# Query and output projections as seven products of blocks, and weight sums moved to GpSimd, in a float32 macaron block

## The chip, the cores and the metric

One core of one Trainium2 chip. The metric is device time in microseconds (us) of one execution: the median of several runs.

## The reference: what is computed

A block with two feed-forward halves around an attention, each with a residual, for 8 samples of 512 tokens by 512 features, all in float32:

```python
x = x + 0.5 * ffn(layernorm(x), w_gate, w_up, w_down)
x = x + attn(layernorm(x), W_q, W_k, W_v, W_o)
x = x + 0.5 * ffn(layernorm(x), w_gate, w_up, w_down)

# ffn: 512 -> 2048 -> 512
h = silu(x @ w_gate) * (x @ w_up)
h = keep the two largest magnitudes of every four of h
return h @ w_down

# attn: 16 query heads and 4 key/value heads of 32 features, rotary positions
Q, K, V = x @ W_q, x @ W_k, x @ W_v
out = softmax(rope(Q) @ rope(K).T / sqrt(32)) @ V
return out @ W_o
```

## The kernel before

**Engines.** TensorE (PE in the profile) multiplies; VectorE (DVE) and ScalarE (ACT) read its banks; [...] SyncE's queue (SP) issues every DMA in one order. A float32 matmul appears as two instructions, so four matmuls are eight rows.

**Stages.** The work is a row of 16 feed-forward blocks (`blocks`, two for each sample), and `ffn` (L503) is the main stream: four chunks of 512 hidden features, two groups each. A group is computed by `woven` (L593) as seven products of quarter blocks in place of eight (a Strassen-Winograd scheme: sums of quarters of the tokens and of the weights are multiplied, the results are added and subtracted by VectorE). A product is four matmuls of 128x128 by 128x256, issued at L604; weights come as 16 quarters ahead of use (`load_quarters`, L106). After a chunk, `keep_two_of_four` (L371) makes the mask on VectorE and three sums on GpSimd (L424 to L429). Then `products` (L513) multiplies two chunks by down weights, in seven products of eight matmuls (L532), which VectorE adds to the tokens (L545). Down weights need sums of quarters; `combine_down` (L469) makes them once, in the first block: it loads `raw` (L473), VectorE adds (L482), and SP stores each sum to DRAM (L483). The sums for gate and up weights are made in the first block as well, by `combine_gu` (L668; additions at L673, stores at L674).

**What goes between.** Layer norms and attentions are generators that the main loop at L1018 advances a step at a time between feed-forward products. Each has a place in the count `n` of feed-forward steps (`sides`, L974): a step runs when `n` has passed its due and its operands are ready by the plan, or when it is 3 steps late. So the order on every engine is written when the kernel is built. The plan keeps a clock for each engine (`at`, L141). VectorE work that can wait stands in three queues (`soon`, urgent; `later`; `for_later`), from which `fill` (L352) issues what fits behind TensorE's clock. `ensure` issues what must be out.

**Attention** (`attention`, L752) for a sample: load `wqkv` (all of W_q, W_k and W_v in one tile), norm and transpose; `projected` (L768) makes keys, then each quarter of the queries by four matmuls of 128x512 (L772), and VectorE rotates each part (a shuffle, two products, an addition); values at L797. Then, for each of the four quarters of the heads, `scores` (L813; four banks `sc` that VectorE reduces to maxima), `exponentials` (L845), `weighted` (L862) and `divided` (L878). At the end the outputs: four matmuls of 128x512 for each 128 tokens (L944), added to the tokens by VectorE (L951) and stored (L952). The four PSUM banks of `sc` and of `st` are one slot; three more banks serve all other products, one serves `ops`. `p_slots` are two SBUF tiles of 1 MB that attention shares with `raw`.

Of the kernel before, what the change touches and what calls it, by code (L numbers as in the profile page):

```python
# [26 lines left out]
def macaron_block(  # L27
# [31 lines left out]
    wap = ctx.enter_context(tc.tile_pool(name="wap", bufs=1))  # L59
    qkvp = ctx.enter_context(tc.tile_pool(name="qkvp", bufs=1))  # L60
# [140 lines left out]
    wa_slots = Slots(wap, "wa", 1)  # L201
# [54 lines left out]
    def layernorm_t(got, tag, src=None, xb=None):  # L256
# [3 lines left out]
        xn = []  # L260
        for t in range(NT):
            xn.append(xnp.tile([P, D], FP, tag=tag, name="xn"))
            if xb is None:
                nc.sync.dma_start(out=xn[t], in_=src[t * P : (t + 1) * P, :])
# [36 lines left out]
        def sums():  # L301
# [3 lines left out]
            got["sums"] = ts = tp.tile([P, 4, 2, HALF], FP, tag="ts", name="ts")  # L305
            got["made"] = [
                later(0.62, partial(nc.vector.tensor_tensor, ts[:, i], a, b, ALU.subtract), at["act"])
# [3 lines left out]
        if xb is None:  # L311
# [19 lines left out]
            if tag == "xf":  # L331
                sums()
# [113 lines left out]

    gu_made, written = {}, {}
# [21 lines left out]
    def combine_down():  # L469

        for c in range(NCH):
# [6 lines left out]
            sums = wa_slots.tile([P, 6, 2, HD2], FP, "sums")  # L478

            def combine(i, name, c=c, quarter=quarter, sums=sums):  # L480
                op = ALU.add if name[2] == "+" else ALU.subtract
                nc.vector.tensor_tensor(sums[:, i], quarter[name[:2]], quarter[name[3:]], op)  # L482
                nc.sync.dma_start(out=combined[c // 2, name][:, c % 2 * 2 : c % 2 * 2 + 2, :], in_=sums[:, i])  # L483

            for i, name in enumerate(SUMS):
                made = later(0.7, partial(combine, i, name), at["pe"], for_later)
            p_slots.used(wa_slots.used(made))
            yield now
        ensure([made])
# [13 lines left out]
    def ffn(b, final, last):  # L503
# [9 lines left out]
        def products(hs, g):  # L513

            operands = []

# [234 lines left out]

    def attention(b):  # L752
        ensure(written[b, 0])
        wa = wa_slots.tile([P, ND, D + 2 * KV], FP, "wqkv")
        for src, col in ((w_k, D), (w_q, 0), (w_v, D + KV)):
            nc.sync.dma_start(
                out=wa[:, :, col : col + src.shape[1]], in_=src.rearrange("(c p) n -> p c n", p=P)
            )
        cs = p_slots.tile([P, 4, S], FP, "cs")
        nc.sync.dma_start(out=cs[:, :2, :], in_=rope.rearrange("a p s -> p a s"))  # L760
        got = {}
# [6 lines left out]
        def projected(dst, col, scale):  # L768

            ps = Bank([P, S], "proj")  # L770
            for k in range(ND):
                nc.tensor.matmul(  # L772
                    out=ps.tile, lhsT=wa[:, k, col : col + P], rhs=xT[:, k, :], start=(k == 0), stop=(k == ND - 1)
                )
            takes("pe", 3.62)
            fill()
            sw = w_slots.tile([P, S], FP, "sw")
            soon(0.65, partial(nc.vector.stream_shuffle, sw, ps.tile, SWAP))
            read = soon(
                0.62, partial(nc.vector.scalar_tensor_tensor, dst, ps.tile, scale, cs[:, 0, :], ALU.mult, ALU.mult)  # L780
            )
            ps.free([read])
            soon(0.65, partial(nc.vector.scalar_tensor_tensor, sw, sw, scale, cs[:, 1, :], ALU.mult, ALU.mult))
            made = soon(0.65, partial(nc.vector.tensor_tensor, dst, dst, sw, ALU.add))
            return [p_slots.used(w_slots.used(made))]

        of_k = projected(kT, D, 1.0)
        yield now
        of_q = []
        for c in range(ND):  # L790
            of_q.append(projected(qT[:, c, :], c * P, 1.0 / math.sqrt(HD)))
            yield now
        ensure(of_q[-1])
        vps = Bank([P, NT, KV], "vps")
        for t in range(NT):
            for k in range(ND):
# [3 lines left out]
                    rhs=wa[:, k, D + KV : D + 2 * KV],  # L800
# [5 lines left out]
        in_xT.remove(got)  # L806
        nc.scalar.copy(v, vps.tile)
        vps.free(end=takes("act", 0.6, pe_heard()))
        wo = wa_slots.tile([P, ND, D + 2 * KV], FP, "wo")
        nc.sync.dma_start(out=wo[:, :, :D], in_=w_o.rearrange("(c p) n -> p c n", p=P))  # L810
        yield partial(when, of_k + of_q[0])
# [88 lines left out]
        ensure(of_k + of_q[0])  # L900
# [33 lines left out]
        xts = []  # L934
        for t in range(NT):
            xts.append(xnp.tile([P, D], FP, tag="xa", name="xt"))
            nc.sync.dma_start(out=xts[t], in_=tokens[b][1][t * P : (t + 1) * P, :])
        out_of = divided(*last)
        yield partial(when, out_of)
        ensure(out_of)  # L940
        for t, xt in enumerate(xts):
            y = Bank([P, D], "y")
            for k in range(ND):
                nc.tensor.matmul(  # L944
                    out=y.tile, lhsT=qT[:, k, t * P : (t + 1) * P], rhs=wo[:, k, :D], start=(k == 0), stop=(k == ND - 1)
                )
            takes("pe", 3.65)
            fill()

            def add(t=t, xt=xt, y=y):  # L950
                nc.vector.tensor_tensor(xt, y.tile, xt, ALU.add)  # L951
                nc.sync.dma_start(out=tokens[b][2][t * P : (t + 1) * P, :], in_=xt)  # L952

            made = [soon(0.62, add)]
            y.free(made)
            if t == NT - 1:
                ensure(made)
# [132 lines left out]
```

## Time and profile before

| what | value |
|---|---|
| median of 3 runs (lowest to highest) | 3263.59 us (3262.45 to 3264.31) |
| the profiled execution: its time | 3262.97 us |
| its span, first to last instruction | 3261.2 us |
| mean granted TensorE clock | 0.997 |
| TensorE, VectorE, ScalarE, GpSimd busy | 3200.0, 2261.7, 1196.7, 564.3 us |
| VectorE rows of 128x512 float32 | 0.67 to 0.80 us each |
| 256 KB of gate/up weights, issue to landing (median) | 3.3 us |

How to read it: durations are of one profiled execution. A row of the timeline gives its start, how long it lasted, the engine, the line, the operation, what it writes and reads, and how many instructions are merged in it; in brackets stands idle time before it and who ended it. Ends of matmuls are modelled and overlap the next start, so how long TensorE takes for a piece is read from start to start. The view of waits names who waited for whom: total, times, longest. One block of the main stream is some 200 us long, the first block is the first 125 us or so together with the sums of weights.

### The profile page before, as it was taken

What the parts mean: (1) busy time and instruction counts of PE and PEld (TensorE: products, weight loads), DVE (VectorE), ACT (ScalarE), POOL (GpSimd) and SP (SyncE); (2) the same over time, 40 slices, a digit from 0 to 9 for tenths busy, and PEclk for the clock granted to TensorE, in tenths of its full rate; (3) what the DMA queues carried; (4) which work ended last, traced back from release to release, by engine and by line L of the source; (5) the groups of instructions that cost most, each with busy time, mean ns of one, the idle gap of its engine ahead of it and who ended that gap; (6) DMA issues with size and microseconds to landing.
All of it is one profiled execution on the core that took longest, in us unless ns stands there. A gap on an engine that the chain in (4) does not pass through costs nothing.

```text
span 3261.2 us, 43693 instructions
## 1 busy us (share of the span) xinstructions
PE 3200.0 (98%) x15880; PEld 2316.7 (71%) x15880; DVE 2261.7 (69%) x4892; ACT 1196.7 (37%) x1686; POOL 564.3 (17%) x868
## 2 busy tenths in 40 slices
PE   7999999999999999999999999999999999999999
PEld 5786667766667677766776668766766678666886
DVE  6767775778577775776578865777577765777554
ACT  2222552155324451354314442155325542255221
POOL 0221112210130112110221111211120121201120
PEclk9999999999999999999999999999999999999999
DMA  7563334543433444334453345433533436234451
GB/s 244 196 221 108 116 127 145 174 130 101 158 134 126 136 139 162 133 118 138 143 172 129 110 154 176 140 119 117 196 97 115 155 126 210 91 117 135 156 174 46
DMA packets 249285, 463.21 MB, mean 142 GB/s; under 512 B 24432, under 2 KB 64368, under 8 KB 248304
## 3 DMA queue, kind: packets, MB, share of 16 engines
q1 hardware_dynamic: 249072, 460.42, 42.9%
q8 instruction: 127, 2.08, 0.3%
q14 instruction: 86, 0.70, 0.1%
HBM read 421.53 MB, written 38.80 MB: 141 GB/s over the span
## 4 chain that ended last, share of the span: by engine, by line
PE 92%; DVE 4%; DMA 2%; ACT 1%; issue 0%; POOL 0%; SPq 0%; DVEq 0%; ACTq 0%
PE x L604 25%; PE y L532 23%; PE v L604 12%; PE z L604 6%; PE proj L772 4%; PE sc L817 4%; PE st L850 4%; PE ops L865 4%; PE y L944 3%; PE tr L244 1%; PE gu L579 1%; DMA xn<-x 1%; DVE nm L157 1%; PE den L883 1%; PE vps L797 1%; PE y L562 1%
## 5 line engine op out<-in xcount | busy, mean ns | idle before, releaser
L604 PE MATMUL x<-ts,w 128*128 128x256 f32 x3000 | 721.5, 383 | 10.7 <-DVE corner L618 9.2
L604 PEld LDWEIGHTS x<-ts,w 128*128 128x128 f32 x3000 | 560.0, 190 | 165.5 <-issue 50.1
L532 PE MATMUL y<-wd,h 128*128 128x256 f32 x1984 | 457.3, 385 | 12.0 <-DVE h L418 6.3
L532 PEld LDWEIGHTS y<-wd,h 128*128 128x128 f32 x1984 | 375.8, 192 | 101.3 <-issue 32.0
L858 ACT ACTIVATE p<-st 128x2048 f32<-128x2048 f32 x128 | 239.6, 1872 | 400.7 <-PE st L855 233.2
L424 POOL TENSOR_TENSOR e<-h 128x512 f32<-128x512 f32 x62 | 89.3, 1440 | 1615.4 <-DVE h L418 1442.7
L157 DVE TENSOR_REDUCE nm<-sc 128x1 f32<-128x512 f32 x512 | 320.2, 681 | 68.8 <-PE sc L817 66.9
L532 PE MATMUL y<-wd,e 128*128 128x256 f32 x1488 | 337.3, 381 | 0.2 <-PE den L883 0.2
L545 DVE SCALAR_TENSOR_TENSOR x<-y,x 128x512 f32<-128x512 f32 x372 | 241.9, 683 | 130.2 <-PE y L532 128.6
L532 PEld LDWEIGHTS y<-wd,e 128*128 128x128 f32 x1488 | 279.7, 190 | 62.3 <-issue 18.7
L236 ACT ACT_TABLE_LOAD x216 | 277.1, 1283 | 4.5 <-PEq L1079 0.7
L224 ACT COPY row<-x 128x512 f32<-128x512 f32 x212 | 124.1, 585 | 392.5 <-PE x L604 392.1
L157 DVE TENSOR_TENSOR p<-p 128x512 f32<-128x512 f32 x384 | 248.4, 700 | 10.4 <-PE ops L865 10.4
L653 ACT ACTIVATE h<-x 128x256 f32<-128x256 f32 x125 | 47.5, 380 | 558.1 <-PE x L604 525.0
L604 PE MATMUL v<-xT,w 128*128 128x256 f32 x1000 | 241.5, 385 | 5.7 <-DVE corner L226 5.7
L604 PE MATMUL v<-ts,w 128*128 128x256 f32 x1000 | 240.1, 383 | 1.1 <-DVE h L157 1.1
L604 PE MATMUL x<-xT,w 128*128 128x256 f32 x1000 | 240.5, 383 | 0.0
L604 PE MATMUL z<-xT,w 128*128 128x256 f32 x1000 | 240.0, 383 | 0.0
L604 PEld LDWEIGHTS v<-xT,w 128*128 128x128 f32 x1000 | 187.3, 191 | 57.3 <-issue 13.2
L604 PEld LDWEIGHTS x<-xT,w 128*128 128x128 f32 x1000 | 185.3, 190 | 57.4 <-issue 30.6
L604 PEld LDWEIGHTS v<-ts,w 128*128 128x128 f32 x1000 | 186.8, 190 | 54.8 <-issue 20.8
L604 PEld LDWEIGHTS z<-xT,w 128*128 128x128 f32 x1000 | 185.8, 190 | 52.6 <-issue 22.9
(106 smaller groups left out, 4010.4 us busy)
## 6 DMA issues: line engine op xcount, KB each, us to landing
w<-gu SPq DMA_DIRECT2D x472, 256.0 KB, 3.3
w<-in_w_gu SPq DMA_DIRECT2D x394, 256.0 KB, 3.3
wd<-wd SPq DMA_DIRECT2D x155, 512.0 KB, 3.8
wd<-in_w_down SPq DMA_DIRECT2D x124, 256.0 KB, 5.0
x<-x SPq DMA_DIRECT2D x64, 256.0 KB, 2.6
xn<-x SPq DMA_DIRECT2D x64, 256.0 KB, 7.0
x<-in_x SPq DMA_DIRECT2D x32, 256.0 KB, 3.4
gu<-w SPq DMA_DIRECT2D x32, 256.0 KB, 2.6
```

Of the source, the lines that this page charges most:

```text
L157: self.does()
L224: nc.scalar.copy(dst, src)
L236: nc.scalar.activation(dummy[:, 1:2], dummy[:, 0:1], f)
L532: nc.tensor.matmul(out=y.tile[:, t, :], lhsT=part[:, t * P : (t + 1) * P], rhs=operands[i][:, n, :], start=(n == 0), stop=(n == 3),)
L545: nc.vector.scalar_tensor_tensor(to, y.tile, 0.5 * sign, to, ALU.mult, ALU.add)
L604: nc.tensor.matmul(out=bank.tile[:, m, :], lhsT=lhs[:, m, k, :], rhs=rhs[:, k, :], start=(first and m == 0 and k == 0), stop=(k == 1), ski ...
L772: nc.tensor.matmul(out=ps.tile, lhsT=wa[:, k, col : col + P], rhs=xT[:, k, :], start=(k == 0), stop=(k == ND - 1))
L817: nc.tensor.matmul(out=sc[:, kv, :], lhsT=qT[rows, c, t * P : (t + 1) * P], rhs=kT[rows, :], start=True, stop=True)
L850: nc.tensor.matmul(out=st[:, kv, :], lhsT=kT[rows, t * P : (t + 1) * P], rhs=qT[rows, c, :], start=True, stop=False)
L858: nc.scalar.activation(p, st, AF.Exp)
L865: nc.tensor.matmul(out=ops[rows, :], lhsT=v[:, t, rows], rhs=p[:, kv, :], start=(t == 0), stop=(t == NT - 1))
L944: nc.tensor.matmul(out=y.tile, lhsT=qT[:, k, t * P : (t + 1) * P], rhs=wo[:, k, :D], start=(k == 0), stop=(k == ND - 1))
```

## The change

1. *Queries and outputs by seven products.* `seven` replaces the four groups of `projected` for queries and the four output groups: seven products of four matmuls of 128x256, accumulated in three banks of the slot of the scores. Between products of one bank VectorE reads it. Each product takes its own weight tile (256 KB) from a new pool `waq` of four, loaded when an earlier one has been used. `b` blocks and their sums (`ts`, now made for attention too) are the tokens' side; for outputs VectorE makes four sums of `qT`.
2. *Rotation by quarters.* Query parts are rotated where they lie in `qT`, as two rows of 256 tokens at a time; the last part straight from the bank.
3. *Order.* Values are projected before the queries; scores begin when all queries are rotated. The attention has 73 steps instead of 65.
4. *Sums by GpSimd.* `combine_down` uses `nc.gpsimd` for its 20 sums, in two parts at other places of the count (11 to 18, 22 to 32, instead of 9 to 25). A new `combine_qo` (36 to 48) makes four sums for W_q and four for W_o by GpSimd, once, and stores them to DRAM.
5. *Buffers.* `wqkv` becomes a tile for keys and values; the four token tiles of an attention become one. The host lays W_q and W_o out in quarters.

```diff
-        for c in range(NCH):
+        for c in range(2 * g, 2 * g + 2):
             raw = p_slots.tile([P, 4, D], FP, "raw")
             nc.sync.dma_start(out=raw, in_=w_down[c])
...
+            for i, name in enumerate(SUMS):
                 op = ALU.add if name[2] == "+" else ALU.subtract
-                nc.vector.tensor_tensor(sums[:, i], quarter[name[:2]], quarter[name[3:]], op)
-                nc.sync.dma_start(out=combined[c // 2, name][:, c % 2 * 2 : c % 2 * 2 + 2, :], in_=sums[:, i])
...
+                total = waq.tile([P, 2, HD2], FP, tag="waq", name="total")
+                nc.gpsimd.tensor_tensor(total, quarter[name[:2]], quarter[name[3:]], op)
+                nc.sync.dma_start(out=combined[g, name][:, c % 2 * 2 : c % 2 * 2 + 2, :], in_=total)
...
+    def combine_qo():
+        for which, how in (("q", Q_SUMS), ("o", O_SUMS)):
+            both = [p_slots.tile([P, 4, 2, HALF], FP, "both") for _ in range(2)]
+            w = [both[q // 4][:, q % 4] for q in range(8)]
+            for q in range(4):
+                nc.sync.dma_start(out=w[q].rearrange("p a b -> p (a b)"), in_=flat(qo_raw[which][q]))
+            there = at["pe"] + 12.0
+            yield lambda: there
+            for to, a, b, op in how:
+                nc.gpsimd.tensor_tensor(w[to], w[a], w[b], op)
+            nc.sync.dma_start(out=qo_sums[which], in_=both[1])
+            yield now
...
+        def seven(lhs, rhs, take):
+            sc = sc_slots.tile([P, N_KV, 2, HALF], FP, "seven")
+            x, v, z = (sc[:, i] for i in range(3))
+            for i, bank in enumerate((x, v, x, v, x, z, x)):
+                w = weights.popleft()
+                for m in range(2):
+                    for k in range(2):
+                        nc.tensor.matmul(
+                            out=bank[:, m, :],
+                            lhsT=lhs(w, i, m, k),
+                            rhs=rhs(w, i, k),
+                            start=(i in (0, 1, 5) and m == 0 and k == 0),
+                            stop=(k == 1),
+                            skip_group_check=True,
+                        )
+                takes("pe", 1.83)
+                if coming_qo:
+                    weights.append(load_qo(*coming_qo.popleft()))
+                fill()
+                entries = take(i, bank)
+                for entry in entries:
+                    sc_slots.used(entry)
+                yield partial(when, entries)
+                takes("pe", 0.0, ensure(entries) + TOLD)
...
+            if i < 3:
+                return [copy((left, corner, right)[i])]
+            if i == 6:
+                return rotate(below, 0, bank)
+            to, j = ((right, 1), (corner, 1), (left, 0))[i - 3]
+            entry = into(to)
+            rotate(to, j)
+            return [entry]
...
-        for t, xt in enumerate(xts):
-            y = Bank([P, D], "y")
-            for k in range(ND):
-                nc.tensor.matmul(
-                    out=y.tile, lhsT=qT[:, k, t * P : (t + 1) * P], rhs=wo[:, k, :D], start=(k == 0), stop=(k == ND - 1)
-                )
-            takes("pe", 3.65)
...
+        def take_output(i, bank):
+            def add(to):
+                nc.vector.tensor_tensor(to, bank, to, ALU.add)
+                if i >= 5:
+                    for t in (0, 1) if i == 5 else (2, 3):
+                        nc.sync.dma_start(out=tokens[b][2][t * P : (t + 1) * P, :], in_=xt[:, t, :])
+            return [soon(0.62, partial(add, (left, corner, right, right, corner, left, below)[i]))]
...
-    sides = [(9, 25, 3 * NCH, combine_down, None, None)]
+    sides = [(11, 18, 6, partial(combine_down, 0), None, None), (22, 32, 6, partial(combine_down, 1), None, None), (36, 48, 4, combine_qo, None, None)]
```

## The prediction

> **What bounds the kernel now.** I read the busy times and the 40 slices first, then TensorE's own waits, then the stages that the change touches in the timeline.
>
> ```profile
> PE 3200.0 (98%) x15880; PEld 2316.7 (71%) x15880; DVE 2261.7 (69%) x4892; ACT 1196.7 (37%) x1686; POOL 564.3 (17%) x868
> ...
> PE   7999999999999999999999999999999999999999
> ...
> PE 92%; DVE 4%; DMA 2%; ACT 1%; issue 0%; POOL 0%; SPq 0%; DVEq 0%; ACTq 0%
> ```
>
> TensorE (PE) is busy nine tenths or more in every slice but the first, and the chain that ended last is 92% TensorE. So taking a matmul away shortens the run as long as the engines that feed TensorE don't turn the gap into a wait. The waits of TensorE alone tell how much waiting there is (columns: total us, times, longest):
>
> ```profile
> PE x L604 <- DVE corner L618: 9.2, 4, 3.7
> ...
> PE sc L817 <- DVE nm L157: 6.9, 7, 1.4
> PE y L532 <- DVE h L418: 6.3, 2, 3.3
> PE v L604 <- DVE corner L226: 5.7, 1, 5.7
> ```
>
> They are few, and the long ones lie in the first block. TensorE's timeline shows stops of 3.74 us (before 54.75), 5.74 (81.19), 3.33 (101.34) and 2.95 (118.57), 15.8 us in all, all released by VectorE (DVE). After each, TensorE runs slower for a while: the eight instructions at 54.75 take 3.44 us, where the same group takes 1.89 elsewhere. That adds 1.55, and in the same way about 1.9, 2.0 and 2.0 us after the other three: 7.4. The first block loses 23 us that way. In the stages that the change rewrites there is no TensorE wait at all:
>
> ```profile
> 261.62 3.60 PE L772 MATMUL proj<-xT,wqkv 128*128 128x512 f32 x8
> 265.05 3.62 PE L532 MATMUL y<-wd,h 128*128 128x256 f32 x16
> 268.51 3.60 PE L772 MATMUL proj<-xT,wqkv 128*128 128x512 f32 x8
> 271.94 1.89 PE L604 MATMUL x<-ts,w 128*128 128x256 f32 x8
> 273.67 3.60 PE L772 MATMUL proj<-xT,wqkv 128*128 128x512 f32 x8
> ```
>
> Starts count here, since ends overlap: a projection group (four 128x512 matmuls, each two instructions) lasts 265.05 - 261.62 = 3.43 us, a feed-forward group of four 128x256 lasts 273.67 - 271.94 = 1.73 us. The output groups at L944 run from 499.03 to 502.46, again 3.43.
>
> [...] the slow groups follow exactly the four long stops. [...]
>
> ```profile
> 78.54 1.71 POOL L427 TENSOR_TENSOR e<-h 128x512 f32<-128x512 f32 x1
> 79.05 1.49 DVE L157 TENSOR_TENSOR h<-h,corner 128x256 f32<-128x256 f32 x1
> ```
>
> The VectorE product has a mean of 0.44 us, and takes 1.49 while GpSimd works.
>
> **The change, part by part.** Sums are made against the profiled execution's 3262.97 us (span 3261.2), 0.6 below the median 3263.59.
>
> 1. *Fewer products.* Queries: four groups of 3.43 = 13.72 us per sample become seven of 1.73 = 12.11. Outputs the same. The saving is 1.61 us a time, 16 times (8 samples, two projections): **25.8 us**, all on the path, because TensorE sets the end there. Weight loads stay in step (190 ns each, beneath matmul halves of 216 ns). Keys and values keep their matmuls (one group of 3.43, and 16 of 128x128); values only move ahead of the queries.
>
> 2. *VectorE per sample.* Removed: 16 query instructions and 4 output additions. Added: 4 sums of xT, 3 copies, 3 additions, 4 rotations of 4 (shuffle, two products, addition), 4 sums of the attention output, 7 output additions: 37 against 20. Rows of 128x512 take 0.67 to 0.73 us, so 17 x 0.69 = 11.7 us a sample, 94 in all; VectorE goes from 2262 to about 2340 us (72%). I put it beside TensorE's work at nothing: in 270 to 290 us, amid the query stage, VectorE is busy 12.4 of 20, in 500 to 520, amid the outputs, 5.4 of 20. If that cover is gone, all 94 could come onto the path (rival 3).
>
> 3. *The new wait.* Each of the 112 products of the seven goes into a bank that VectorE must first have read: copy or addition (0.69 us) behind the product. [...] In the built program's instruction order each of the seven is followed by at least one feed-forward group (1.73 us; often 3.45), so about 1 us is left over for a reader; rotations (about 2.6 us) are queued behind the addition that the next product waits for, but ahead of the one after it. The trace doesn't show this wait in these stages. Lower end: the same scheme in the feed-forward part waits 17.5 us in all at L604, 9.5 of it in the two first-block stops, the other 8 over some 826 products, 0.01 each, 1 us for 112. Below nothing is excluded: no wait stands in these stages that could go. Upper end: one stop of 1.38 us (the usual one before scores) in each of 16 phases: 22. I take **+6**: one 0.75 us stop, as before 909.80, in every second phase.
>
> 4. *Sums of down weights on GpSimd.* Twenty instructions at L482 (0.757 us, 15.1 together) leave VectorE in the first block; GpSimd gets them at 1.27 to 1.44 us (rows L427, L424), 25 to 29 us, and 8 more for query and output weights. [...] from 76.3 to 83.3 us five GpSimd instructions stretched VectorE by about 0.73 + 1.07 + 1.55 = 3.35 us, 0.67 each. 20 x 0.67 = 13.4, so VectorE's net relief is about 2 us. What changes more is the order of transfers on SP. The first stop came from weights issued at 41.16 that landed at 50.8 (in the chain, 7.91 us of that load), just behind a raw load of 1 MB:
>
> ```profile
> 40.64 0.42 SPq L473 DMA_DIRECT2D raw<-in_w_down  x1
> 41.16 2.32 SPq L114 DMA_DIRECT2D w<-in_w_gu  x4
> 43.57 3.28 SPq L483 DMA_DIRECT2D wd<-sums  x4
> ```
>
> In the changed order the second raw load stands behind those four. So I take away the first stop with its slow group (3.74 + 1.55 = 5.3) and half of the third (5.3 / 2 = 2.7), which had five L482 rows just ahead of the instruction awaited: **-8**. The second and fourth I leave: there `h` and mask work is late, and GpSimd now adds to it. Ends: -23 (all stops go) and +13 [...].
>
> 5. *What else is queued.* SP's stores of GpSimd's sums wait for GpSimd, five in a row (some 7 us), and gate/up loads emitted behind them wait as long; in the changed order one such row precedes the loads of the fifth and of the sixth group. Covered by a group's 12 us (seven of 1.73), else in the +13. In attention four large weight loads become 16 of 256 KB, 12 more a sample, about 0.5 us of SP each, past gate/up loads that run up to 16 quarters ahead. Each weight is loaded four products ahead, four times at least 3.46 = 13.8 us, against 3.3 us to land: hidden. The norm's ScalarE and GpSimd steps stay; its small GpSimd chain may stand behind two or three sums (about 4 us) once, within its 13 steps. Scores now wait for all four query parts instead of the first; feed-forward groups fill that: nothing.
>
> Sum: 3262.97 - 25.8 + 6 - 8 = 3235.2; against the median **3236 us**.
>
> **Rivals.**
> 1. *The first block's stops all vanish.* -25.8 - 23 + 3 gives 3217. For it: VectorE released every one. [...]
> 2. *The pairwise exchange eats most of the gain.* A stop of 1.38 us in every phase (22 us) and 4 us off the first block leaves 3263 - 25.8 + 22 - 4 = 3255. For it: VectorE already makes scores wait 1.4 us at a time. Against: no wait in these stages now.
> 3. *VectorE becomes the bound around the rotations and seven pairwise readers* (slower). Each sample adds 11.7 us of VectorE work; the mask steps it pushes back must be done before the down products. It decides from 27% of the 94 us on the path (25.8 / 94; 0.2% slower needs 34%); at half: 3263 - 25.8 + 47 = 3284. For it: slices where VectorE is at eight tenths. Against: 12.4 and 5.4 of 20 us where the work is put.
> 4. *No net change*: a fifth to a third of those 94 us on the path, 3263.
>
> **How the numbers follow.** About 0.2% (6.5 us) is what a measurement of this kernel can tell from no change, so faster is below 3257 and slower above 3270. Forecast (3226 to 3247) 0.60; rival 1 (below 3226) 0.13; rival 2 (3247 to 3257) 0.14; rival 4 0.06; rival 3 0.07. Faster: 0.60 + 0.13 + 0.14 = 0.87. The range runs to the first two rivals: 3216 to 3256, with some 0.17 outside.
>
> **What would show it.** Right: `seven` groups 1.73 us apart, TensorE busy down by about 26 us, hardly any `PE seven <- DVE` wait, no stop before 55 us, VectorE near 2340. Wrong: `PE seven` or `PE y <- DVE h` waits of tens of us (rivals 2, 3), half-clock groups in the first block still, or GpSimd rows above 1.7 us with VectorE rows doubled beside them.

## The result, and the profile after

| | before | after |
|---|---|---|
| median of 5 runs each, on one chip (lowest to highest) | 3263.58 us (3261.74 to 3264.31) | 3293.52 us (3289.91 to 3296.36) |
| ratio, with its 95% interval | | 1.0093 (1.0078 to 1.0107) |
| the profiled execution: its time, its span | 3262.97, 3261.2 us | 3289.91, 3288.1 us |
| mean granted TensorE clock | 0.997 | 0.996 |

The changed kernel is 0.9% slower, where 0.8% faster was predicted. From the page of the changed kernel, the same three parts as were shown of before (busy times, TensorE's slices, the chain that ended last):

```profile
PE 3194.5 (97%) x16264; PEld 2391.3 (73%) x16264; DVE 2380.0 (72%) x5018; ACT 1160.9 (35%) x1636; POOL 614.0 (19%) x896
...
PE   8999999999999999999999999999999999999999
...
PE 84%; DVE 10%; DMA 2%; ACT 2%; issue 1%; POOL 1%; SPq 0%; DVEq 0%; ACTq 0%; POOLq 0%
```

The first slice rose from 7 to 8: the first block gained. Everywhere else the slices look as before; a digit is too coarse for a loss of 1%. The chain tells more: TensorE's share fell from 92% to 84%, VectorE's rose from 4% to 10%. TensorE's waits in the changed kernel (total us, times, longest):

```profile
PE sc L923 <- DVE nm L158: 15.4, 13, 2.0
PE x L608 <- DVE corner L622: 14.0, 7, 5.1
PE x L608 <- ACT row L224: 7.6, 2, 6.0
...
PE ops L971 <- ACT p L964: 4.8, 6, 1.8
...
PE seven L834 <- DVE qT L158: 2.0, 5, 0.5
```

The wait that the change adds, `seven`, is only 2.0 us. What grew is a wait between instructions that the diff doesn't touch: scores waiting for maxima (`sc <- nm`) went from 6.9 us in 7 stops to 15.4 in 13. The stage that was rewritten looks as the prediction said, groups of 1.73 us from start to start, one stop of 0.24:

```profile
279.78 1.89 PE L834 MATMUL seven<-xT,waq 128*128 128x256 f32 x8
281.50 3.62 PE L536 MATMUL y<-wd,e 128*128 128x256 f32 x16
285.36 1.99 PE L834 MATMUL seven<-ts,waq 128*128 128x256 f32 x8 [0.24 <-DVE qT L158]
287.19 3.62 PE L536 MATMUL y<-wd,e 128*128 128x256 f32 x16
```

The first block has no stop at 54.75 us any more; one of 3.58 comes at 67.08, with a group of usual length behind it:

```profile
52.98 1.89 PE L608 MATMUL x<-xT,w 128*128 128x256 f32 x8
54.70 1.89 PE L608 MATMUL v<-ts,w 128*128 128x256 f32 x8
...
67.08 1.99 PE L608 MATMUL x<-ts,w 128*128 128x256 f32 x8 [3.58 <-DVE corner L622]
```

The sums there of GpSimd (POOL), a VectorE row beside them, and SP's stores (GpSimd's, VectorE's and SP's timelines of the changed kernel):

```profile
58.40 6.28 POOL L489 TENSOR_TENSOR total<-raw 128x512 f32<-128x512 f32 x4
```

```profile
60.65 4.57 DVE L677 TENSOR_TENSOR w<-w 128x512 f32<-128x512 f32 x3 [1.67 <-DMA w<-in_w_gu]
```

```profile
38.54 1.84 SPq L115 DMA_DIRECT2D w<-in_w_gu  x4
40.48 8.60 SPq L490 DMA_DIRECT2D wd<-total  x5
...
50.60 0.55 SPq L481 DMA_DIRECT2D raw<-in_w_down  x1
```

Three VectorE sums take 4.57 us beside GpSimd's, where three of the mean length of before take 2.05 (3 x 0.684): the kind of cost that the prediction counted from 76.3 to 83.3 us of the kernel before (3.35 us; the trace has four GpSimd instructions there, not five, so 0.84 each and 16.8 for twenty). SP stands 8.60 us over five stores (some 7 were expected). The four weight loads at 38.54 now go ahead of the second load of `raw`, where they stood just behind it before. The first block is shorter in spite of the two costs.

### The profile page after: what moved, and what is told of

It reads as the page before. It is cut to its first block, busy times and chain, and to the rows that moved or that the text cites. A ratio compares the mean times of both kernels' runs of the same rounds, so it can differ in the third digit from the quotient of the medians.

```text
span 3288.1 us, 44735 instructions
## 1 busy us (share of the span) xinstructions
PE 3194.5 (97%) x16264; PEld 2391.3 (73%) x16264; DVE 2380.0 (72%) x5018; ACT 1160.9 (35%) x1636; POOL 614.0 (19%) x896
## 4 chain that ended last, share of the span: by engine, by line
PE 84%; DVE 10%; DMA 2%; ACT 2%; issue 1%; POOL 1%; SPq 0%; DVEq 0%; ACTq 0%; POOLq 0%
PE x L608 23%; PE y L536 21%; PE v L608 11%; PE z L608 6%; PE seven L834 5%; PE sc L923 4%; PE ops L971 4%; PE st L956 4%; DVE nm L158 2%; PE den L989 1%; PE gu L583 1%; PE tr L244 1%; DVE p L158 1%; ACT p L964 1%; PE vps L866 1%
## 5 line engine op out<-in xcount | busy, mean ns | idle before, releaser
L158 DVE TENSOR_TENSOR p<-p 128x512 f32<-128x512 f32 x384 | 257.9, 726 | 13.4 <-PE ops L971 13.4
```

What stands on the lines that cost most here:

```text
L158: self.does()
```

## Where the time went, stage by stage

The waits listed don't add up to the loss, since many are under the limit of what that view lists, and a stop shows in the length of the next group too (287.19 - 285.36 = 1.83 us behind the stop of 0.24 above, where 1.73 is usual). So I took every group of TensorE from its own start to the next one's, and subtracted what such a group usually takes: 0.216 us for each 128x256 instruction, 0.429 for 128x512, 0.134 for one of `sc`, and so on for each shape, as the undisturbed groups of the trace show. What is subtracted is called work here, the remainder stops. The middle of an attention runs from its first `sc` to its last `den`; its first part, "the first four scores", ends where the first product for exponentials (`st`) starts. Feed-forward groups that lie in a stage count in it. All eight attentions together, us:

| stage | before: work | stops | after: work | stops |
|---|---|---|---|---|
| up to the first keys, first block included | 217.6 | 32.5 | 217.7 | 21.1 |
| keys, values, queries | 274.8 | 0.7 | 341.2 | 8.4 |
| middle: the first four scores of each attention | 189.7 | 16.7 | 174.2 | 40.2 |
| middle: the rest | 1535.9 | 68.4 | 1437.8 | 91.0 |
| outputs | 198.0 | 1.1 | 274.3 | 1.7 |
| between the attentions | 682.7 | 12.4 | 627.4 | 22.3 |
| sum | 3098.7 | 131.8 | 3072.6 | 184.7 |

Some 31 us complete the spans: what lies ahead of TensorE's first group, and everything from the start of its last one on. Of the middles' stops more than 40 us in either kernel are remainders of under 0.3 us at a change of group, which come back in every kernel; the comparison is what counts. The work fell by 26.1 us, as predicted. The stops grew by 53: 46 in the middles (23.5 in the first scores, 22.6 in the rest), 10 between the attentions, 8 at the queries, less 11 up to the first keys. The columns of work show something else: the stages of queries and outputs *grew*, by 66.4 and 76.3 us, although their own products shrank by 26. So 169 us of other work, nearly all of it feed-forward, moved into them: 114 out of the middles and 55 from between.

How that makes stops is seen at the first scores of one attention. In the kernel before (TensorE's timeline):

```profile
295.83 1.14 PE L817 MATMUL sc<-kT,qT 32*128 32x512 f32 x8
296.90 3.72 PE L532 MATMUL y<-wd,e 128*128 128x256 f32 x16
300.55 1.14 PE L817 MATMUL sc<-kT,qT 32*128 32x512 f32 x8
301.62 3.72 PE L532 MATMUL y<-wd,e 128*128 128x256 f32 x16
305.27 1.14 PE L817 MATMUL sc<-kT,qT 32*128 32x512 f32 x8
```

and in the changed kernel, the same scores of the same attention:

```profile
298.91 1.14 PE L923 MATMUL sc<-kT,qT 32*128 32x512 f32 x8
299.98 1.99 PE L608 MATMUL x<-xT,w 128*128 128x256 f32 x8
302.66 1.14 PE L923 MATMUL sc<-kT,qT 32*128 32x512 f32 x8 [0.68 <-DVE nm L158]
303.73 1.99 PE L608 MATMUL v<-ts,w 128*128 128x256 f32 x8
306.41 1.14 PE L923 MATMUL sc<-kT,qT 32*128 32x512 f32 x8 [0.68 <-DVE nm L158]
```

VectorE's side of the changed one:

```profile
300.12 2.48 DVE L158 TENSOR_REDUCE nm<-sc 128x1 f32<-128x512 f32 x4 [0.41 <-PE sc L923]
303.87 2.48 DVE L158 TENSOR_REDUCE nm<-sc 128x1 f32<-128x512 f32 x4 [1.26 <-PE sc L923]
```

A score group needs all four banks of its slot, so it may start only when the four reductions of the one before are done, which take 2.48 us here. Before, 16 instructions of a down product stood between two scores and hid that; after, 8 instructions are left. Other groups had been drawn to the queries and outputs; it is also another moment of the feed-forward block, so this one place doesn't show how much of its difference is the one and how much the other. A score comes every 3.75 us with 2.80 us of TensorE work: 0.95 lost a time. VectorE isn't full here (it stands 1.26 us of the 3.75); each engine waits for the other.

## The experiments

The table has the measured numbers of all runs; middle columns as above. "Steps" are those of one attention. Ratios are against the kernel before on the same chip.

| kernel | steps | median us | ratio (95% interval) | first scores: work / stops | rest: work / stops | queries, outputs: stops | between: stops |
|---|---|---|---|---|---|---|---|
| before | 65 | 3263.58 | 1 | 190 / 16.7 | 1536 / 68.4 | 1, 1 | 12 |
| after | 73 | 3293.52 | 1.0093 (1.0078, 1.0107) | 174 / 40.2 | 1438 / 91.0 | 8, 2 | 22 |
| e3_busywork | 65 | 3264.23 | 1.0006 (0.9997, 1.0014) | 190 / 16.7 | 1536 / 68.3 | 2, 1 | 14 |
| e2_squeeze | 65 | 3261.23 | 0.9996 (0.9988, 1.0005) | 216 / 7.1 | 1491 / 75.1 | 1, 1 | 16 |
| e5_squeeze_more | 65 | 3270.50 | 1.0024 (1.0015, 1.0033) | 221 / 6.8 | 1408 / 91.4 | 2, 1 | 6 |
| e1_pace | 73 | 3277.40 | 1.0047 (1.0032, 1.0062) | 147 / 36.3 | 1485 / 94.5 | 8, 2 | 9 |
| e4_norm_first | 73 | 3280.03 | 1.0057 (1.0042, 1.0072) | 174 / 40.0 | 1438 / 91.0 | 8, 2 | 14 |
| e10_values_last | 72 | 3286.81 | 1.0071 (1.0059, 1.0084) | 176 / 27.1 | 1453 / 100.5 | 8, 2 | 22 |
| e6_pairs | 67 | 3285.52 | 1.0069 (1.0056, 1.0083) | 189 / 18.5 | 1502 / 73.6 | 34, 10 | 27 |
| e7_pairs_norm | 67 | 3266.16 | 1.0008 (1.0000, 1.0016) | 172 / 30.2 | 1533 / 69.1 | 24, 9 | 7 |
| e8_gpsimd_sums | 65 | 3248.06 | 0.9957 (0.9944, 0.9971) | 190 / 16.7 | 1536 / 68.0 | 1, 1 | 13 |
| e9_fewer_steps | 66 | 3258.46 | 0.9986 (0.9978, 0.9994) | 200 / 18.0 | 1511 / 72.1 | 1, 11 | 26 |
| e11_all | 65 | 3256.63 | 0.9981 (0.9974, 0.9988) | 204 / 20.5 | 1529 / 66.0 | 10, 10 | 26 |
| e12_outputs_only | 69 | 3246.15 | 0.9952 (0.9939, 0.9966) | 182 / 21.0 | 1491 / 80.6 | 1, 1 | 5 |

The theory is *crowding*. Between two products of the seven a step ends, and at least one feed-forward group goes there. The stock of such groups is fixed, so fewer are left for the middle, where every step of an attention needs a cover (TensorE work of other parts that hides the wait for VectorE or ScalarE). Its rivals: VectorE's added work by itself (rival 3 of the prediction), the order of loads ahead of the norm, and the order of values and queries.

### VectorE's added work alone

e3_busywork is the kernel before with 17 additions a sample that nothing reads, 10 behind the query projections and 7 behind the outputs:

```diff
+    def busywork(n):
+        for _ in range(n):
+            soon(0.62, partial(nc.vector.tensor_tensor, idle, idle, idle, ALU.add))
...
+            busywork(3 if c < 2 else 2)
...
+            busywork(1 if t == 0 else 2)
```

Expected: 

> The kernel before, with 17 extra VectorE additions of 128x512 a sample into a tile that nothing reads: ten behind the query projections, seven behind the output groups, as many as the change adds; 136 in all, 94 us of VectorE. Nothing else is changed. Theory B (added VectorE work): the score stages' excess rises from 85 to 120 us or more, and the time to 3290 or above. Theory A (pace): up by less than 8 us, below 3272, and the middle keeps its 85 us of excess. Theory C: slower by 10 to 40 us, since the queue of VectorE work is planned anew.

Its page shows VectorE busy 92 us longer than before (2353.9 against 2261.7), almost the 94 of the prediction:

```profile
PE 3202.7 (98%) x15880; PEld 2319.8 (71%) x15880; DVE 2353.9 (72%) x5028; ACT 1196.8 (37%) x1687; POOL 571.9 (18%) x868
```

The time moved by 0.06%, within its interval of none, and no stage's stops by over 2 us. VectorE's load as such isn't the cause, and rival 3's 94 us on the path fall. The additions of e3 depend on nothing and nothing waits for them, so this run says nothing of rotations and readers that TensorE waits for.

### Crowding without the sevens

e2_squeeze and e5_squeeze_more change only the pace of the kernel before. `WEIGHTS` gives each step its share of an attention's time; a larger one for norm, projections and outputs leaves less to the middle:

```diff
-    WEIGHTS = [0.5] * (NORM + ND + 2) + [0.7] * (NT + 1) + [0.9] * (ND * (2 * NT + 1) + 1) + [0.5] * NT
+    WEIGHTS = [0.674] * (NORM + ND + 2) + [0.7] * (NT + 1) + [0.9] * (ND * (2 * NT + 1) + 1) + [0.674] * NT
```

Expected of e2 (0.674): 

> The kernel before with one edit: the weight of its norm, projection and output steps is 0.674 instead of 0.5, so that the score and exponential steps get the width that they have in the changed kernel. Theory A (pace): the score stages' excess rises from 85 us to about 130, and the time from 3263.6 to about 3300 to 3310. Theory B (added VectorE work): no change beyond 8 us, 3256 to 3272. Theory C (any new order loses): slower by 10 to 40 us, like every change of the plan.

Expected of e5 (0.9): 

> The kernel before, with 0.9 as the weight of its norm, projection and output steps. 0.674 left the middles of the attentions (first score to last sum) with 1708 us of TensorE work, own and interleaved, where the kernel before has 1726 and the changed one 1612; in the built order 0.9 takes about as much feed-forward work out of the middles as the change does. Theory A2 (crowding: fewer feed-forward groups lie between the score steps, so the same VectorE and ScalarE work stands behind less TensorE work): the middles' excess rises from 85 us to 115 to 140, and the time from 3262.5 to about 3290 to 3310. Rival F (it is the seven products' own waits and reordered reads, not the crowding): the middles stay at 80 to 95 us, the time at 3258 to 3268.

e2 hardly narrowed the middle (1708 us of work instead of 1726) and so told little: no loss, where its forecast by pace had 3300 to 3310 us. e5 took the middle's work to 1629, near the changed kernel's 1612. The rest of the middle then stops for 91.4 us, as after (91.0), without one product of the seven; the first scores, which kept more work between them (221), stop for 6.8. From e5's list of waits:

```profile
PE ops L865 <- ACT p L858: 8.9, 8, 1.8
...
PE st L850 <- DVE nm L157: 4.9, 9, 0.7
```

The first of these was 0.4 us in one stop in the kernel before: too little TensorE work is left to cover ScalarE's exponentials. In the changed kernel it is 4.8 us. So the loss in the rest of the middle, 23 of the 46 us, can be made by the pace alone. The sum is a miss, though: the middles as a whole stop for 98 us, not the 115 to 140 of the forecast, and the median is 3270.5, just above the rival's 3258 to 3268. It rose 7 us, less than 23, because the first scores and the stretches between gained.

### Pace, loads and order in the changed kernel

e1_pace gives the changed kernel's added steps smaller shares (0.371 for 0.5), so that norm, projections and outputs have together what they had before:

```diff
-    WEIGHTS = [0.5] * (NORM + 2 + 8) + [0.7] * (NT + 1) + [0.9] * (ND * (2 * NT + 1) + 1) + [0.5] * 8
+    WEIGHTS = [0.371] * (NORM + 2 + 8) + [0.7] * (NT + 1) + [0.9] * (ND * (2 * NT + 1) + 1) + [0.371] * 8
```

Expected: 

> The changed kernel with one edit: the weights that divide an attention's stretch of the count among its steps are 0.371 instead of 0.5 for the norm, projection and output steps, so that the score and exponential steps get the width they had before (sum 48.3 as before, 52.3 in the changed kernel). Theory A (pace: the attention's middle is squeezed, so VectorE's score work falls on fewer feed-forward groups): excess TensorE time in the score stages falls from 131 us to near the 85 of before, and the time from 3293 to about 3250 to 3260. Theory B (the added VectorE instructions themselves push mask work and score readers back): the middle keeps at least 120 us of excess, and the time stays within 10 us of 3293. Theory C (neither: any new order loses what the written order of before happened to fit): the middle moves by 10 to 30 us either way, without relation to its width.

Theory A, by pace, missed: the middle's stops stayed (131), and the 16 us that the run gained came from elsewhere, 13 of them between the attentions (22 to 9). The work in queries and outputs hardly fell (615.5 to 611.7 us): smaller shares didn't narrow these stages, as if each step kept its feed-forward group. This run doesn't fit a rule by the sum of work either: its rest has 1485 us of work and yet 94.5 of stops.

e4_norm_first puts the norm's token loads ahead of the four first weight tiles:

```diff
-        weights = deque(load_qo(*coming_qo.popleft()) for _ in range(4))
         got = {}
-        yield from layernorm_t(got, "xa", tokens[b][1])
+        norm = layernorm_t(got, "xa", tokens[b][1])
+        loaded = next(norm)
+        weights = deque(load_qo(*coming_qo.popleft()) for _ in range(4))
+        yield loaded
+        yield from norm
```

Expected: 

> The changed kernel, with the first four query weight tiles loaded behind the norm's token loads instead of ahead of them. In the changed kernel VectorE stood 8.1 to 8.3 us before two norms until their tokens landed, and TensorE stopped 5.1 and 6.0 us behind it and then ran at half clock. Theory D (these loads in front of the tokens cost the stops between attentions): the idle time of the norm's statistics (34.7 us) falls to about the 21 of before, the excess between attentions from 22 us to about 12, the time by some 8 to 12 us to about 3283. Rival: the tokens are late because of the stores of the attention before them, and the time stays within 4 us of 3293.

In the changed kernel, SP issues four weight tiles ahead of the tokens, VectorE stands at the head of its queue for the tokens (8.26 us), and TensorE waits for VectorE (5.13 us; the group behind that takes 3.78 us, at a granted clock of 0.50):

```profile
891.36 0.47 SPq L791 DMA_DIRECT2D waq<-in_w_q  x1
891.87 2.86 SPq L791 DMA_DIRECT2D waq<-sums_q  x3
...
895.18 3.30 SPq L267 DMA_DIRECT2D xn<-x  x4
...
901.68 0.70 DVE L273 BATCH_NORM_STATS2 st<-xn 128x6 f32<-128x512 f32 x1 [8.26 <-DMA xn<-x]
...
908.04 3.78 PE L608 MATMUL x<-ts,w 128*128 128x256 f32 x8 [5.13 <-DVE corner L622]
```

In e4 at the same place (VectorE's rows, then TensorE's):

```profile
899.13 0.69 DVE L273 BATCH_NORM_STATS2 st<-xn 128x6 f32<-128x512 f32 x1 [5.64 <-DMA xn<-x]
```

```profile
905.49 3.68 PE L608 MATMUL x<-ts,w 128*128 128x256 f32 x8 [2.51 <-DVE corner L622]
```

The stop is half as long; between the attentions 22 us became 14, and the median fell 13.5 us. The middle is unchanged to 0.2 us, so this is a loss apart from crowding. Over all norms VectorE waits 34.7 us for tokens in the changed kernel, 21.0 in the one before and 14.3 in e4, so the order of these loads accounts for all of the added wait, against the rival of its forecast.

e10_values_last projects values behind the queries, as before. In the changed kernel the last rotation's four VectorE instructions stand right ahead of the first scores' reductions; the values' 3.6 us of TensorE work now lie there. The edit moves the block from `vps = Bank(...)` to the copy into `v` behind `yield from seven(...)`, with one step less.

Expected: 

> The changed kernel with the values projected behind the queries again, as before the change, so that 16 small matmuls (3.6 us) stand between the last rotation and the first scores; the widths are nearly those of the changed kernel (180 and 1465 us against 179 and 1450). Theory V (the first scores wait because the last rotation, four VectorE instructions, is still in VectorE's queue): excess at the first scores falls from 40 us to 17 to 25, time from 3293 to about 3273. Theory A2 alone (the width decides): excess at the first scores stays at 35 us or more, time within 6 us of 3290.

The first scores' stops fell from 40 to 27 at nearly the same work (176), so the order is a part of the loss there. The rest's rose from 91 to 100.5, and the median fell 7 us only, between the two forecasts.

### Fewer steps in the changed kernel

e6_pairs lets two products go in one step, four steps for seven; e7 is e6 with e4's loads and shares of 0.4:

```diff
-                yield partial(when, entries)
-                takes("pe", 0.0, ensure(entries) + TOLD)
+                owing.extend(entries)
+                if i % 2 or i == 6:
+                    yield partial(when, list(owing))
+                    takes("pe", 0.0, ensure(owing) + TOLD)
+                    owing.clear()
```

Expected of e6: 

> The changed kernel, with the seven products issued as (0, 1), (2, 3), (4, 5), (6): four steps for a projection instead of seven, so fewer feed-forward groups are drawn between them and the middles keep about as many as before (in the built order 1708 against 1743 us of the kernel before and 1628 of the changed one, by the same count). Arithmetic and VectorE work are those of the changed kernel. Theory A2 (crowding): the middles' excess falls from 131 to 85 to 95 us, and the time from 3293 to about 3250. Rival F: pairs of dependent products give VectorE less time, the waits at the seven grow by 10 us or more, the middles stay above 120, and the time stays above 3285.

Expected of e7: 

> Pairs as in the other run, with the norm's token loads ahead of the weight tiles, and 0.4 in place of 0.5 as the weight of the norm, projection and output steps. Theories A2 and D together: excess in the middles about 85 us, between attentions about 13, in the first block 18; TensorE's own work 26 us less than before: 3262.5 - 26 - 13 + 5 = about 3230, faster than both kernels. Rival F: above 3275.

The middle's stops came back to 92 and 99 us. But the wait that step 3 priced comes true at the queries, where an odd product must wait at once for the rotations of the pair before. From e6's list of waits:

```profile
PE seven L835 <- DVE qT L158: 16.9, 7, 3.1
...
PE seven L835 <- DVE xt L1072: 6.4, 10, 1.7
```

Queries stop for 34 and 24 us and outputs for 10 and 9: as large a loss at another place. So e7 came to 3266.16, not to the 3230 of its forecast.

e9_fewer_steps therefore pairs the outputs only, saves four steps in the attention's norm (scales and transposes two by two), takes e4's loads, and gives the first scores a share of 1.0; e11 adds e10's order:

```diff
+                if tag == "xa" and t % 2 == 0:
+                    continue
                 yield now
...
-    WEIGHTS = [0.5] * (NORM + 2 + 8) + [0.7] * (NT + 1) + [0.9] * (ND * (2 * NT + 1) + 1) + [0.5] * 8
+    WEIGHTS = [0.5] * (NORM - 4 + 2 + 8) + [1.0] * (NT + 1) + [0.9] * (ND * (2 * NT + 1) + 1) + [0.5] * 5
```

Expected of e9: 

> The changed kernel with its products one by one for queries, in pairs for outputs, with the norm's four scalings and four transposes of an attention in two steps each, the tokens loaded ahead of the weight tiles, and 1.0 in place of 0.7 for the first scores. The products, sums and rotations are those of the changed kernel; only the steps into which an attention is cut are fewer (66 instead of 73), so feed-forward groups move from the projections back among the scores. By the built order the first scores get 203 us of TensorE work (before 192, changed 179), the rest of the middles 1526 (before 1551, changed 1450). Theory A2 (crowding): excess in the first scores about 12 us instead of 40, in the rest about 72 instead of 91; with 18 in the first block, 13 between and 16 at the projections the time is about 3240. Rival (the waits come with the seven products, wherever the groups lie): excess in the middles above 115 us, time above 3265.

Expected of e11: 

> Both together: fewer steps, tokens first, output pairs, values behind the queries. Widths by the built order 206 and 1545 us. Theory A2: excess 10 us in the first scores and 70 in the rest, time about 3235 to 3242, no more than 5 us from the run with fewer steps. If the values' place matters by itself: 5 to 15 us below that run. If neither: above 3265.

With 66 and 65 steps the middles stop for 90 and 87 us, near the 85 of the kernel before, with all sevens in place; so the sevens as such don't make the middles wait. Several things were changed at once here, and which of them brought the middles back isn't separated. The medians are 3258.46 and 3256.63, not the 3240 or so that I forecast for e9 and e11: paired outputs stop for 11 and 10, and between the attentions there are 26 us of stops where e4 has 14. The norm's paired steps have a part in that, such as this stop of e9, a pair of transposes behind ScalarE's scaling:

```profile
892.61 1.97 PE L244 MATMUL tr<-ident,xn 128*128 128x128 f32 x8 [3.51 <-ACT xn L291]
```

e11's further edit put 10 us at the queries, and the intervals of the two overlap. Eight steps can be saved, but each saving that I tried has a wait of its own.

### Parts of the change by themselves

e8_gpsimd_sums is the kernel before with the sums of down weights alone on GpSimd, in the two parts of the changed kernel:

```diff
-                nc.vector.tensor_tensor(sums[:, i], quarter[name[:2]], quarter[name[3:]], op)
+                total = sums[:, i]
+                nc.gpsimd.tensor_tensor(total, quarter[name[:2]], quarter[name[3:]], op)
...
-    sides = [(9, 25, 3 * NCH, combine_down, None, None)]
+    sides = [(11, 18, 6, partial(combine_down, 0), None, None), (22, 32, 6, partial(combine_down, 1), None, None)]
```

Expected: 

> The kernel before, with the twenty sums of down weights made by GpSimd in the two parts of the changed kernel (written to the tile of before, which has six places); attention unchanged. If the changed kernel's 13 us gain in the first block come from this part: excess there 30 to about 18 us, time about 3250. Rival: [...] 3258 to 3268.

It gains 15.2 us (3263.25, the median before on that chip, to 3248.06). Stops before 130 us fall from 30.5 to 15.4, every other stage keeps its stops within 1 us. The edit moves the sums to another engine and also to other places of the count: four weight loads go out at 37.57, ahead of the second load of `raw` at 47.70, as in the changed kernel. How much of the gain is the engine and how much this order no run tells. At 55 us TensorE runs on, as in the changed kernel:

```profile
53.71 1.89 PE L602 MATMUL v<-ts,w 128*128 128x256 f32 x8
55.44 1.89 PE L602 MATMUL x<-ts,w 128*128 128x256 f32 x8
```

e12_outputs_only does half of the rest: e8's sums, e4's order of loads, outputs by seven in single steps, but queries by full products as before (their weights in four tiles by output columns):

```diff
+        for c in range(ND):
+            w = weights.popleft().rearrange("p (c n) -> p c n", c=ND)
+            ps = Bank([P, S], "proj")
+            for k in range(ND):
+                nc.tensor.matmul(out=ps.tile, lhsT=w[:, k, :], rhs=xT[:, k, :], start=(k == 0), stop=(k == ND - 1))
...
-    WEIGHTS = [0.5] * (NORM + 2 + 8) + [0.7] * (NT + 1) + [0.9] * (ND * (2 * NT + 1) + 1) + [0.5] * 8
+    WEIGHTS = [0.5] * (NORM + ND + 2) + [0.7] * (NT + 1) + [0.9] * (ND * (2 * NT + 1) + 1) + [0.5] * 8
```

Expected: 

> This kernel does half of the change: sums of down weights by GpSimd and the outputs by seven single products, as in the changed kernel, tokens loaded ahead of the weights; but the queries come from the 16 full products of the kernel before, each followed by one rotation. An attention has 69 steps, between the 65 before and the 73 after; in the built order, TensorE work of about 211 us stands in the middle of an attention, where 218 did before and 204 after. Work without any stop is 3129.5 - 12.7 = 3117 us. Theory (crowding: the middle loses the feed-forward groups that the added steps take): about half of the added stops come back, so the middles stop for 85 + 46 x 54 / 115 = about 107 us over all eight (98 to 115), the first scores for over 17, the stages of queries and outputs for under 2; between the attentions 14, first block 18: 3117 + 18 + 3 + 1 + 107 + 14 = 3260 of span, 3255 to 3268 measured. Rival (the queries by seven are the whole cause, by the rotations that they leave in front of the first scores): the middles stop for 82 to 92 us as before, 3240 to 3248 measured. Second rival (sevens that share the score banks are the cause wherever they stand, the ones for outputs too): waits at the products for outputs, over 8 us there.

The middles stop for 101.6 us: in the range of crowding (98 to 115), above that of the rival by queries (82 to 92). The sum of the forecast was off elsewhere, most of all between the attentions (5 instead of 14 us), so the median is 3246.15 instead of 3255 to 3268. That time lies in the range of the first rival; only the stage tells the two apart. From its list of waits:

```profile
PE st L939 <- DVE nm L158: 8.4, 8, 1.5
PE sc L906 <- DVE nm L158: 8.2, 9, 1.4
```

No `seven` wait is in that list, and the outputs stop for 1 us, which answers the second rival. The kernel is 0.5% faster than the one before, and can't be told from e8 (the intervals of their ratios overlap): it has 12.4 us less work than e8, and 11.2 more of stops (127.3 against 116.1 in all). None of the kernels with seven products came out clearly below e8, which has none.

## Why the prediction was wrong, step by step

1. *Fewer products, -25.8.* Right: TensorE's work fell by 26.1 us.

2. *VectorE's added work at nothing.* Right for its load: e3 shows 92 us of it hidden. VectorE grew to 2380 instead of 2340 us, for the most part because some rows got longer than before: the sums of gate/up weights in the first block take 0.953 us instead of 0.684, the sums of tokens (`ts`) take 0.80 us instead of the 0.69 to 0.71 before, the sums of `p` 0.726 instead of 0.700.

3. *The wait at the sevens, +6.* Near in size: 7.7 at the queries and 0.6 at the outputs. Only 2.0 of that is listed as the sevens' own wait; 3.3 is values that wait for the keys to be read (`vps <- kT`), a wait that neither the kernel before nor e10, where values follow the queries, has in its list. The argument of this step has the failure in it, though. It said that "each of the seven is followed by at least one feed-forward group" and took these groups as given.

4. *Sums by GpSimd, -8.* Right in sign, too small: -12.9 in the first 130 us after, -15.1 in e8. I took away one stop and a half of the four (3.74, 5.74, 3.33, 2.95 us). What is left after is 3.58 at 67.08, and nothing else above 1.6; the granted clock from 12 to 130 us is 1.00, where it was 0.93 before and the slow groups behind four stops cost 7.4 us. So the second and the fourth stop, which I left, went as well. That the first would go by the order of loads fits the trace, but e8 has the engine in it too.

5. *Other queues at nothing.* This is the step that failed, twice. "Scores now wait for all four query parts instead of the first; feed-forward groups fill that: nothing" is the larger: they fill it, but most of them are taken from the middle, where 114 us of work went missing and 46 us of stops came. The prediction has no term for that. I had read the order of one stage, where the groups arrive, and not the sum over the stage that they leave. And "In attention four large weight loads become 16 of 256 KB" was judged by their own landing; I didn't ask what stands behind them on SP, the norm's tokens, for which VectorE waited 8.26 us at one norm (34.7 at all norms, 21.0 before) with the mask work of the feed-forward block behind it: 10 us between the attentions, 8 to 9 of it gone in e4.

The sum by stages: -26.1 (products) - 11.4 (up to the first keys) + 7.7 (queries) + 46.1 (middles) + 0.6 (outputs) + 9.9 (between) = +26.8, against 26.9 between the spans. The rivals: none named this mechanism. Rival 3 had the sign, and at half of its 94 us a size of +21 against the measured +30. Its reason, VectorE's load, is excluded by e3; the rotations that it names have a part in the first scores (e10).

*What the crowding theory rests on.* In the kernels with sevens the middle's stops follow the number of steps: 87 us at 65 steps, 90 at 66, 92 and 99 at 67, 102 at 69, 128 at 72, 131 at 73 in three kernels. e5 makes the loss in the rest with 65 steps, by pace. What fits both, and e1 as well, is how the covers are dealt out. In each middle, take every place where other TensorE work lies between two pieces of the attention's own work (320 places in each kernel), and count those with the shortest cover that occurs, one group of eight instructions (1.73 us):

| kernel | places with the shortest cover | stops of the middles, us |
|---|---|---|
| e2_squeeze | 30 | 82 |
| e9_fewer_steps, e11_all | 32, 35 | 90, 87 |
| before, e8_gpsimd_sums, e6_pairs | 36, 36, 36 | 85, 85, 92 |
| e12_outputs_only | 39 | 102 |
| e5_squeeze_more, e7_pairs_norm | 46, 46 | 98, 99 |
| e10_values_last | 50 | 128 |
| after, e4_norm_first, e1_pace | 54, 54, 56 | 131, 131, 131 |

e1 gave the middles 20 us more work than the changed kernel has, but 56 of its places kept the shortest cover. This count was made afterwards, and no run was built to test it. The stops at the shortest covers grew from 22.9 us before to 46.2 after, half of the loss in the middles.

What stays open: the other half, most of it at 13 places with a longer cover that stop for over 1 us (30.9 us in all), where the kernel before has 4 (6.3 us); how much of the first scores' 23.5 us is the order of rotations and how much is the smaller cover (e10 gave 13 back, but moved 9.5 to the rest); and why stops between the attentions range from 5 to 27 us in kernels whose norms differ little.

## What to carry to other kernels

Filler work that hides a wait is a stock: when an edit adds steps to one stage, ask which stage gives up the groups, and compare the work per stage, and the shortest covers, of the built order before and after. A saving of 26 us in products was lost to 46 us in a stage whose own products the diff leaves as they were. And take an edit with several parts apart early: one part of this one, the sums by GpSimd at their new places, is a gain of 15 us by itself.

## What the runs showed of the hardware

*Half clock after short stops.* In the kernel before, the prediction saw slow groups behind four long stops; the granted clock there was 0.55 (54.75 to 58.03 us), 0.50 (81.19 to 84.77), 0.63 (101.34 to 105.96) and 0.63 (118.57 to 123.13). In the changed kernel a slow group also follows three shorter stops in a row (TensorE's timeline):

```profile
1716.83 1.14 PE L923 MATMUL sc<-kT,qT 32*128 32x512 f32 x8 [0.68 <-DVE nm L158]
1717.90 1.99 PE L608 MATMUL v<-xT,w 128*128 128x256 f32 x8
1721.34 1.14 PE L923 MATMUL sc<-kT,qT 32*128 32x512 f32 x8 [1.45 <-DVE nm L158]
1722.41 1.99 PE L608 MATMUL x<-ts,w 128*128 128x256 f32 x8
1726.39 1.14 PE L923 MATMUL sc<-kT,qT 32*128 32x512 f32 x8 [1.98 <-DVE nm L158]
1727.46 3.60 PE L608 MATMUL z<-xT,w 128*128 128x256 f32 x8
```

The last group takes 3.60 us instead of 1.89 or 1.99, at a granted clock of 0.53 (1727.46 to 1730.86). The same comes again at 2120 to 2132 us, behind stops of 0.68, 1.80 and 1.98: a clock of 0.62 from 2130.36 to 2134.91, where eight instructions of `sc` take 2.06 us instead of 1.14 and the group behind them 2.73. At 1727 us the three stops cost another 1.7 us behind them.

Nor does the length of one stop decide. Slow groups follow stops of 3.33 and 2.95 us in the kernel before, and one follows a stop of 2.51 us in e4 (905.49, 3.68 us for the group); groups of usual length, 1.99 us, follow one of 2.55 us in e8 (65.06) and the one of 3.58 in the changed kernel (67.08, at a clock of 1.00).

*VectorE's sums beside GpSimd's.* In the first block GpSimd's 20 sums take 1.45 us each, and VectorE's 32 sums at L677 rise from a mean of 684 ns to 953, up to 1756 for one. The groups of the two in the changed kernel, from the first 150 us and from the whole run (busy us, mean ns; idle before, releasers):

```profile
L677 DVE TENSOR_TENSOR w<-w 128x512 f32<-128x512 f32 x32 | 29.7, 953 | 7.0 <-DMA w<-in_w_gu 6.2 <-DMA wd<-total 0.5
```

```profile
L489 POOL TENSOR_TENSOR total<-raw 128x512 f32<-128x512 f32 x20 | 28.6, 1454 | 49.5 <-DMA raw<-in_w_down 33.8 <-DMA wd<-total 15.7
```

The engines' busy times say that nothing was won (VectorE gave away 14.3 us of sums and got 8.6 back in these rows alone, and GpSimd worked 28.6 longer), and yet TensorE's stops in the first 130 us fell from 30.5 to 17.6 us. So busy time isn't what explains the gain; that it is when VectorE is free, or when loads are issued, is likely but not shown.
